# Turning the attention probabilities of layer 2: TensorE transposes replaced by 32x32 squares on VectorE and transfers within SBUF

## The chip, the cores and the metric

The kernel runs on one core of a Trainium2 chip, in one launch. A core has five engines that run side by side, each through its own instruction list in order: TensorE (PE in the profile, with PEld for its weight loads), VectorE (DVE), ScalarE (ACT), GpSimd (POOL) and SyncE (SP, which here only issues DMA transfers). An engine waits when an instruction needs a result of another engine or of a transfer. The metric is the device time of one execution in microseconds (us); of three runs of the kernel before, the median is 1385.75 us (1385.43 to 1386.89).

## What is computed

Four blocks, one after the other, on a residual stream x of 4 x 256 tokens of 512 floats. Each block normalises x and adds an attention and a feed-forward part to it. All is 32-bit floats. The change concerns the attention of block 2 alone:

```python
def _L2_attn_ref(hidden_states, Wqkv, Wo):       # 4 x 256 tokens, 32 query heads, 8 key heads, 128 wide
    qkv = jnp.einsum('bsh,oh->bso', hidden_states, Wqkv)
    ...
    xq = _apply_rope(xq, cos, sin)
    xk = _apply_rope(xk, cos, sin)
    ...
    scores = jnp.einsum('bqhd,bkhd->bhqk', xq, xk) * scale
    scores = jnp.where(causal, scores, -1e30)
    probs = jax.nn.softmax(scores, axis=-1)
    out = jnp.einsum('bhqk,bkhd->bqhd', probs, xv)
    return jnp.einsum('bsd,hd->bsh', out, Wo)

xn = _layernorm(x)
x = x + _L2_attn_ref(xn, Wqkv, Wo) + _L2_ffn_ref(xn, ...)
```

## The kernel before, in words

The work of blocks 2 and 3 is written as a list of tasks for TensorE (`layers_2_and_3`). One task is a group of eight 128x256 float matmul passes (two passes for each matmul that the program names). Seven tasks make a product of 2x2 blocks by seven multiplications (`seven`): four PSUM banks X, Y, Z and W are opened by tasks 0 to 3, and tasks 4 to 6 add to three of them. Around each group ScalarE copies two banks out (`u` at line 1330, `z` at 1335), and VectorE adds them together (1332, 1340, 1350) and either rotates queries and keys (1411, 1413; GpSimd adds the halves at 1420) or adds to the residual stream (1454).

There are sixteen rounds, called quads; a round makes the queries of the next quad (7 tasks), the output product of the one before (7 tasks) and in some rounds new keys and values (7 more tasks). In between, the attention of four units runs. A unit, here called a head h, is one key head with two query heads of one batch: 64 heads in all, each spread over m tasks, m being 3 to 6 and in the first rounds more. The helper `run` takes the tasks in order; each task is a slot, and `after(k, f)` puts an operation k slots later. All engines but SP keep exactly this written order (`manual_schedule`).

For head h, counted from its first slot:

- slot 0, before the task: `scores` puts four matmuls on TensorE (lines 1755, 1759): 128 later queries against 256 keys and 128 earlier queries against 128 keys, for both query heads.
- slot 0: `masked`, four VectorE instructions that add the causal mask, store the negated scores in SBUF and keep their extreme (line 1773).
- slot 1: `exponentials`, four ScalarE instructions (1789), in place.
- slot 2: `normalise`, a reciprocal on VectorE (1800) and two products on GpSimd (1803), in place.
- slot m//3 of the next head: `transposes`, six 128x128 transposes on TensorE into banks T and V (1811 to 1814), and `copies`, two ScalarE copies to SBUF (1821, 1822).
- slot 2m//3 of the next head: `values`, the product with the values (1828, 1829), and a slot later `gathered`, a ScalarE copy of the result to SBUF (1837).

The probabilities of later and earlier queries lie in two tiles, p1 and p0, of two buffers each; q0 and q1, their transposes, have one buffer each. Weights come by transfers that SP issues; the tile framework gives all transfers of SP and ScalarE eight completion counters in turn, and a transfer waits until the one before it on its counter has landed.

Of the kernel before, what the change touches and what calls it, by code (L numbers as in the profile page):

```python
# [21 lines left out]
F32 = mybir.dt.float32  # L22
# [9 lines left out]
P = 128  # L32
# [24 lines left out]
def block_stack(ctx: ExitStack, tc: tile.TileContext, d: dict, out: bass.AP):  # L57
# [1188 lines left out]
    def layers_2_and_3(w, late):  # L1246
# [8 lines left out]
        with ExitStack() as stack:  # L1255
# [229 lines left out]
            class Layer3:  # L1485
# [29 lines left out]
                def integers(self):  # L1515


                    self.held = xs.tile([P, NC, C], F16, name="w3_h")
                    pk = [lnp.tile([P, C], F32, tag="xn", name=f"pk_{a}").bitcast(I32) for a in range(2)]
                    for a in range(2):  # L1520
                        nc.sync.dma_start(out=pk[a], in_=d["pk3"][:, a, :])

                    def step(a, k):
                        q = sp.tile([P, C], I32, tag="p1", name="nib")
                        nc.vector.tensor_scalar(
                            q, pk[a], 4 * k, 15, ALU.logical_shift_right, ALU.bitwise_and
                        )
                        nc.vector.tensor_copy(self.held[:, 2 * a + k, :], q)

                    return [lambda a=a, k=k: step(a, k) for a in range(2) for k in range(2)]  # L1530
# [233 lines left out]
            def masked(h):  # L1764

                x = heads[h]
                x["p1"] = sp.tile([P, 2, T], F32, tag="p1", name="p1")
                x["p0"] = sp.tile([P, 2, P], F32, tag="p0", name="p0")
                for k in ("nm", "sums", "rs"):
                    x[k] = sp.tile([P, 2, 2], F32, tag=k, name=k)  # L1770
                for part in (1, 0):
                    for e in range(2):
                        nc.vector.tensor_tensor_reduce(  # L1773
                            out=x[f"p{part}"][:, e, :],
                            in0=x[f"s{part}"][:, e, :],
                            in1=cmask if part else cmask[:, P : 2 * P],
                            scale=-1.0,
                            scalar=-NEG,
                            op0=ALU.add,
                            op1=ALU.min,  # L1780
                            accum_out=x["nm"][:, part, e : e + 1],
                        )
# [15 lines left out]
            def normalise(h):  # L1798
                x = heads[h]
                nc.vector.reciprocal(x["rs"], x["sums"])  # L1800
                for part, n in ((1, T), (0, P)):
                    p = x[f"p{part}"]
                    nc.gpsimd.tensor_tensor(p, p, bc(x["rs"][:, part, :], 2, n), ALU.mult)  # L1803

            def transposes(h):


                x = heads[h]
                t0, t1 = ps("T", [P, 2, T], "pT0"), ps("V", [P, 2, P], "pT1")
                for i in range(2):  # L1810
                    nc.tensor.transpose(t0[:, i, 0:P], x["p0"][:, i, :], ident)
                    nc.tensor.transpose(t0[:, i, P:T], x["p1"][:, i, 0:P], ident)  # L1812
                for i in range(2):
                    nc.tensor.transpose(t1[:, i, :], x["p1"][:, i, P:T], ident)
                x.update(t0=t0, t1=t1)

            def copies(h):
                x = heads[h]
                x["q0"] = sp.tile([P, 2, T], F32, tag="q0", name="q0", bufs=1)
                x["q1"] = sp.tile([P, 2, P], F32, tag="q1", name="q1", bufs=1)  # L1820
                nc.scalar.copy(x["q0"], x["t0"])  # L1821
                nc.scalar.copy(x["q1"], x["t1"])  # L1822

            def values(h):
                x = heads[h]
                v = x["kt"][:, 1, :]
                av = x["av"] = ps("V", [P, 2, T], "av2")
                nc.tensor.matmul(av, lhsT=v[:, 0:P], rhs=x["q0"], start=True, stop=False)  # L1828
                nc.tensor.matmul(av[:, :, P:T], lhsT=v[:, P:T], rhs=x["q1"], start=False, stop=True)  # L1829

            attended = {}

            def gathered(h):
                x = heads.pop(h)
                i, j = x["c"]
                o = tile2("o", 8, f"o2_{h}")
                nc.scalar.copy(o, x["av"])  # L1837
                attended.setdefault(x["quad"], {})[f"a{i + 1}{j + 1}"] = o

            def piece(h, k, m):  # L1840


                if h >= 1 and k == m // 3:
                    transposes(h - 1)
                    copies(h - 1)
                if h >= 1 and k == 2 * m // 3:
                    values(h - 1)
                    after(1, lambda: gathered(h - 1))
# [14 lines left out]
            def run(tasks):  # L1863

                for task in tasks:
                    h, at, m = beats.pop(slot[0], (None, 0, 0))
                    if h is not None and at == 0 and h < 4 * QUADS:
                        scores(h)
                        after(0, lambda h=h: masked(h))
                        after(min(1, m - 1), lambda h=h: exponentials(h))  # L1870
                        after(min(2, m - 1), lambda h=h: normalise(h))
                    task()


# [446 lines left out]
```

## Time and profile before

| what | value |
|---|---|
| median of three runs | 1385.75 us |
| the profiled execution, its own time | 1389.1 us |
| its span from first to last instruction | 1387.2 us |
| TensorE busy, of the span | 1347.8 us (97%) |
| VectorE, ScalarE, GpSimd busy | 62%, 38%, 55% |
| stretch from 530 to 1250 us (attention of block 2): TensorE busy | 717.8 of 720 us |
| the same stretch: VectorE, ScalarE, GpSimd busy | 439.0, 265.8, 469.2 us |
| the two GpSimd products of line 1803, mean | 1067 and 653 ns |
| the two ScalarE copies of lines 1821 and 1822, mean | 585 and 377 ns |
| granted TensorE clock in this stretch | 1.00 |

A group of instructions in the profile is given with its line, its engine, its operation, what it writes and reads, its shape and count, the busy time of the group, the mean of one, and the idle time of the engine before it with what ended that. A timeline line starts with the time from the span's start and the duration, both in us; some neighbouring instructions are merged in it (x8). Matmuls overlap in the array, so the distance between starts, not the duration shown, is what one occupies. A PE line counts the passes of a float matmul, two for each; a transpose is one pass. Of a matmul the profile names the output, then the moving and the stationary tile.

### The profile page before, as it was taken

To read this page: it belongs to the slowest core of one execution; us is meant where nothing else is said; L and a number is where in the kernel's file an instruction comes from. 1 tells how busy PE (TensorE), PEld (TensorE's weight loads), DVE (VectorE), ACT (ScalarE), POOL (GpSimd) and SP (SyncE) were. 2 spreads that over 40 slices of the span, in tenths; PEclk is the share of its full clock that TensorE was granted. 3 is DMA by queue.
4 is the path that set the end of the run, shared out by engine and by line. 5 is a ranking of instruction groups with operands and counts; after the bars stand their busy time and mean duration, and the time that the engine had idled before them with its cause. 6 is when DMAs were issued, how large, how long until landed. Compare 5 with 4: busy or idle time off the path is not lost.

```text
span 1387.2 us, 20593 instructions
## 1 busy us (share of the span) xinstructions
PE 1347.8 (97%) x7460; PEld 1064.6 (77%) x7460; DVE 865.7 (62%) x1905; ACT 525.0 (38%) x1346; POOL 760.8 (55%) x782
## 2 busy tenths in 40 slices
PE   9899999899998999999999999999999999999998
PEld 7566665687445678888888888888888888877887
DVE  7576677488835358545665756655466655758654
ACT  2444435387012213323333333333333344555440
POOL 4455456477645025674776856868658675331410
PEclk9899999999999999999999999999999999999999
DMA  5022213200600022011311203121122000302001
GB/s 199 14 46 47 47 35 92 73 1 19 188 28 16 1 84 77 1 46 38 104 57 46 69 17 103 62 72 40 55 69 101 20 24 1 137 1 114 1 1 61
DMA packets 51317, 76.52 MB, mean 55 GB/s; under 512 B 16538, under 2 KB 24373, under 8 KB 50832
## 3 DMA queue, kind: packets, MB, share of 16 engines
q1 hardware_dynamic: 50288, 74.16, 17.2%
q8 instruction: 59, 0.97, 0.3%
q10 hardware_dynamic: 816, 0.79, 0.2%
q14 instruction: 42, 0.34, 0.1%
q0 software_dynamic: 112, 0.26, 0.1%
HBM read 67.28 MB, written 7.91 MB: 54 GB/s over the span
## 4 chain that ended last, share of the span: by engine, by line
PE 90%; DVE 6%; ACT 2%; issue 1%; POOL 1%; DVEq 0%; ACTq 0%; POOLq 0%
PE m L1396 18%; PE m L1360 15%; PE gu L782 6%; PE dn L745 5%; PE half L287 4%; PE s L1755 4%; PE av L1828 4%; PE m L1382 3%; PE m L1372 3%; PE half L327 2%; PE s L1759 2%; PE av L1829 2%; PE l1o L1033 2%; PE st L449 2%; PE s L386 2%; PE half L479 2%
## 5 line engine op out<-in xcount | busy, mean ns | idle before, releaser
L1803 POOL TENSOR_TENSOR p<-p,rs 128x512 f32<-128x512 f32 (+1 forms) x128 | 107.3, 860 | 147.2 <-DVE rs L1800 136.3
L1789 ACT ACTIVATE p<-p,nm 128x256 f32<-128x256 f32 (+1 forms) x256 | 113.3, 443 | 105.8 <-DVE nm L1773 105.5
L1454 DVE TENSOR_TENSOR x_sb<-x_sb,m 128x512 f32<-128x512 f32 x82 | 56.0, 686 | 82.4 <-PE m L1396 67.3
L1360 PE MATMUL m<-xT,wq_b 128*128 128x256 f32 x448 | 103.9, 380 | 2.5 <-ACT kv L1445 1.4
L1773 DVE CUSTOM_DVE_ANT_0 p<-s,cmask 128x256 f32<-128x256 f32 (+1 forms) x256 | 76.2, 354 | 47.5 <-PE s L1755 45.4
L1420 POOL TENSOR_TENSOR q<-q,t 128x512 f32<-128x512 f32 x64 | 82.2, 1285 | 31.4 <-DVE t L1411 28.1
L1837 ACT COPY o<-av 128x512 f32<-128x512 f32 x64 | 37.5, 586 | 156.5 <-PE av L1829 156.5
L1360 PEld LDWEIGHTS m<-xT,wq_b 128*128 128x128 f32 x448 | 82.1, 190 | 13.0 <-ACT kv L1445 1.8
L1396 PE MATMUL m<-wo_b,o 128*128 128x256 f32 x384 | 89.6, 379 | 0.0
L1411 DVE TENSOR_TENSOR t<-m,rope_sb 64x512 f32<-64x512 f32 (+1 forms) x144 | 86.3, 599 | 2.1 <-POOL q L1420 0.2
L463 POOL TENSOR_SCALAR_AFFINE_SELECT keys<-keys 128x256 f32<-128x256 f32 x128 | 56.7, 452 | 49.9 <-ACT keys L459 43.5
L1343 POOL TENSOR_TENSOR c<-c,z 128x512 f32<-128x512 f32 x28 | 36.5, 1302 | 86.6 <-DVE c L1340 45.9
L1821 ACT COPY q<-pT 128x512 f32<-128x512 f32 x64 | 37.5, 585 | 122.3 <-PE pT L1812 122.2
L802 POOL TENSOR_TENSOR sa<-sa,sb 128x1024 f32<-128x1024 f32 x22 | 62.0, 2823 | 30.7 <-DVE sb L797 30.7
L1396 PEld LDWEIGHTS m<-wo_b,o 128*128 128x128 f32 x384 | 71.3, 190 | 8.8
L745 PE MATMUL dn<-wd,hT 128*128 128x512 f32 x176 | 76.4, 593 | 0.7 <-ACT o L741 0.7
L1360 PE MATMUL m<-x_s,wq_t 128*128 128x256 f32 x320 | 75.4, 380 | 1.2 <-ACT kv L1445 1.1
L459 ACT ACTIVATE keys<-st 128x384 f32<-128x384 f32 x128 | 55.9, 487 | 40.0 <-PE st L449 40.0
L1360 PEld LDWEIGHTS m<-x_s,wq_t 128*128 128x128 f32 x320 | 59.8, 190 | 10.1 <-ACT kv L1445 1.5
L1828 PE MATMUL av<-q,kv 128*128 128x512 f32 x128 | 65.6, 594 | 0.6 <-ACT q L1822 0.6
L1755 PE MATMUL s<-kv,q 128*128 128x256 f32 x256 | 65.8, 379 | 0.0
L745 PEld LDWEIGHTS dn<-wd,hT 128*128 128x128 f32 x176 | 33.2, 190 | 41.1 <-issue 39.5
(337 smaller groups left out, 3448.0 us busy)
## 6 DMA issues: line engine op xcount, KB each, us to landing
wq_b<-in_wq SPq DMA_DIRECT2D x38, 256.0 KB, 3.1
wo_b<-in_wo SPq DMA_DIRECT2D x32, 256.0 KB, 2.6
raw<-in_wo SPq DMA_DIRECT2D x16, 512.0 KB, 3.6
wkv_b<-in_wkv SPq DMA_DIRECT2D x16, 256.0 KB, 2.6
wos_d<-wos_row SPq DMA_DIRECT2D x28, 128.0 KB, 2.7
gate_q<-in_gate_q SPq DMA_DIRECT2D x11, 256.0 KB
up_q<-in_up_q SPq DMA_DIRECT2D x11, 256.0 KB
wq3s_b<-in_wq SPq DMA_DIRECT2D x8, 256.0 KB, 3.1
```

Of the source, the lines that this page charges most:

```text
L745: nc.tensor.matmul(po, lhsT=hT[:, k, t * P : (t + 1) * P], rhs=wd[:, k, :], start=k == 0, stop=k == NBLK - 1,)
L782: nc.tensor.matmul(p[:, half], lhsT=w[:, g, :], rhs=x[half][:, g], start=k == 0, stop=k == 1,)
L802: nc.gpsimd.tensor_tensor(self.a, self.a, self.b, ALU.add)
L1360: nc.tensor.matmul(out[:, i, :], lhsT=b[:, c, i * P : (i + 1) * P], rhs=a[:, c, :], start=start and i == 0 and c == 0, stop=i == 1 and c == 1,
L1396: nc.tensor.matmul(out[:, t, :], lhsT=a[:, c, t * P : (t + 1) * P], rhs=b[:, c, :], start=start and t == 0 and c == 0, stop=t == 1 and c = ...
L1411: nc.vector.tensor_tensor(t2[at], src[of], sin[of], ALU.mult)
L1420: after(1 + 2 * pause, lambda: nc.gpsimd.tensor_tensor(dst, dst, t2, ALU.add))
L1755: nc.tensor.matmul(s1[:, i, :], lhsT=q[:, i, P:T], rhs=kt[:, 0, :], start=True, stop=True)
L1773: nc.vector.tensor_tensor_reduce(out=x[f"p{part}"][:, e, :], in0=x[f"s{part}"][:, e, :], in1=cmask if part else cmask[:, P : 2 * P], scale ...
L1789: nc.scalar.activation(p, p, AF.Exp, bias=x["nm"][:, part, e : e + 1], scale=-1.0, accum_out=x["sums"][:, part, e : e + 1],)
L1803: nc.gpsimd.tensor_tensor(p, p, bc(x["rs"][:, part, :], 2, n), ALU.mult)
L1828: nc.tensor.matmul(av, lhsT=v[:, 0:P], rhs=x["q0"], start=True, stop=False)
```

## The change

The probabilities of a head are turned without TensorE:

- p0 and p1 become two views of one tile p with one buffer: for each of the two query heads 3 x 128 columns (earlier queries' 128 keys, later queries' 256 keys).
- `normalise` scales on ScalarE, four instructions with the reciprocal as a scale per partition, in place of two on GpSimd.
- `transposes` and `copies` go. `turned_blocks` takes their place: one VectorE instruction transposes 32x32 squares of the whole of p into a tile `blocks`, reading every fourth column, so that the four columns that will sit on neighbouring partitions end in four rows of one partition. Four transfers, issued by ScalarE, then move 32 partitions each to all 128 partitions of q, 768 bytes to a partition. It stands at slot max(3, 2m//3) of the head itself; for m = 3 that is the first slot of the next head.
- `values` reads q in its new order and writes the bank in an order of 32 columns; `gathered` puts the columns back in order.
- A scratch tile of the last block's weights (`nib`) uses the rotary's buffer t2, as tag p1 is gone.

```diff
-                        q = sp.tile([P, C], I32, tag="p1", name="nib")
+                        q = tile2("t2", 2, "nib").bitcast(I32).rearrange("p a i -> p (a i)")
...
-                x["p1"] = sp.tile([P, 2, T], F32, tag="p1", name="p1")
-                x["p0"] = sp.tile([P, 2, P], F32, tag="p0", name="p0")
+                p = x["p"] = sp.tile([P, 2, 3, P], F32, tag="p", name="p", bufs=1)
+                p = p.rearrange("p e x k -> p e (x k)")
+                x["p0"], x["p1"] = p[:, :, 0:P], p[:, :, P:]
...
                 nc.vector.reciprocal(x["rs"], x["sums"])
-                for part, n in ((1, T), (0, P)):
-                    p = x[f"p{part}"]
-                    nc.gpsimd.tensor_tensor(p, p, bc(x["rs"][:, part, :], 2, n), ALU.mult)
-
-            def transposes(h):
+                for part in (1, 0):
+                    for e in range(2):
+                        p = x[f"p{part}"][:, e, :]
+                        nc.scalar.activation(p, p, AF.Copy, scale=x["rs"][:, part, e : e + 1])
+
+            def turned_blocks(h):
                 x = heads[h]
-                t0, t1 = ps("T", [P, 2, T], "pT0"), ps("V", [P, 2, P], "pT1")
-                for i in range(2):
-                    nc.tensor.transpose(t0[:, i, 0:P], x["p0"][:, i, :], ident)
-                    nc.tensor.transpose(t0[:, i, P:T], x["p1"][:, i, 0:P], ident)
-                for i in range(2):
-                    nc.tensor.transpose(t1[:, i, :], x["p1"][:, i, P:T], ident)
-                x.update(t0=t0, t1=t1)
-
-            def copies(h):
-                x = heads[h]
-                x["q0"] = sp.tile([P, 2, T], F32, tag="q0", name="q0", bufs=1)
-                x["q1"] = sp.tile([P, 2, P], F32, tag="q1", name="q1", bufs=1)
-                nc.scalar.copy(x["q0"], x["t0"])
-                nc.scalar.copy(x["q1"], x["t1"])
+                blocks = sp.tile([P, 4, 6, 32], F32, tag="blocks", name="blocks", bufs=1)
+                nc.vector.transpose(
+                    blocks, x["p"].rearrange("p e x (i b) -> p b (e x) i", b=4)
+                )
+                q = x["q"] = sp.tile([P, 4, 6, 32], F32, tag="q", name="q", bufs=1)
+                for a in range(4):
+                    nc.scalar.dma_start(
+                        out=q[:, a].rearrange("k m j -> k (m j)"),
+                        in_=blocks[32 * a : 32 * a + 32].rearrange("i b m j -> i b (m j)"),
+                    )
...
-                av = x["av"] = ps("V", [P, 2, T], "av2")
-                nc.tensor.matmul(av, lhsT=v[:, 0:P], rhs=x["q0"], start=True, stop=False)
-                nc.tensor.matmul(av[:, :, P:T], lhsT=v[:, P:T], rhs=x["q1"], start=False, stop=True)
+                q = x["q"].rearrange("p a (e x) j -> p a e (x j)", e=2)
+                av = x["av"] = ps("V", [P, 4, 2, 64], "av2")
+                nc.tensor.matmul(av, lhsT=v[:, 0:P], rhs=q[:, :, :, 0:64], start=True, stop=False)
+                nc.tensor.matmul(
+                    av[:, :, :, 32:], lhsT=v[:, P:T], rhs=q[:, :, :, 64:], start=False, stop=True
+                )
...
-                nc.scalar.copy(o, x["av"])
+                nc.scalar.copy(
+                    o.rearrange("p e (x a j) -> p a (e x) j", x=2, a=4),
+                    x["av"].rearrange("p a e (x j) -> p a (e x) j", x=2),
+                )
...
-                if h >= 1 and k == m // 3:
-                    transposes(h - 1)
-                    copies(h - 1)
                 if h >= 1 and k == 2 * m // 3:
                     values(h - 1)
...
                         after(min(2, m - 1), lambda h=h: normalise(h))
+                        after(max(3, 2 * m // 3), lambda h=h: turned_blocks(h))
```

## The prediction

> **What bounds the kernel now.** I read the page first, then the busy time by stretch, then the waits, and last the timeline of the tightest heads. The page, and the table by stretch for the whole attention of block 2 (columns: stretch, length, then busy time and count of PE, PEld, DVE, ACT, POOL, clock, DMA share, GB/s):
>
> ```profile
> span 1387.2 us, 20593 instructions
> PE 1347.8 (97%) x7460; PEld 1064.6 (77%) x7460; DVE 865.7 (62%) x1905; ACT 525.0 (38%) x1346; POOL 760.8 (55%) x782
> ```
>
> ```profile
> 530.00:1250.00 720.00, 717.78 (x3704) 617.19 (x3703) 438.99 (x1114) 265.78 (x818) 469.22 (x435) 1.00 0.17 55
> ```
>
> TensorE works without a gap in this stretch; the others have 40% or so to spare. The waits of PE there sum to 2.2 us in three places, and the chain that ended last is PE for 90% of the span. So what leaves TensorE here leaves the time, as long as nothing else takes its place. The timeline of one head with m = 3 (start, duration):
>
> ```profile
> 1083.70 1.03 PE L1755 MATMUL s<-kv,q 128*128 128x256 f32 x4
> ...
> 1088.47 0.27 PE L1811 MATMUL pT<-ident,p 128*128 128x128 f32 x1
> 1088.58 0.27 PE L1812 MATMUL pT<-ident,p 128*128 128x128 f32 x1
> ...
> 1089.12 1.89 PE L1360 MATMUL m<-x_s,wq_t 128*128 128x256 f32 x8
> ...
> 1090.85 1.02 PE L1828 MATMUL av<-q,kv 128*128 128x512 f32 x2
> ...
> 1092.14 1.03 PE L1755 MATMUL s<-kv,q 128*128 128x256 f32 x4
> ```
>
> Starts tell what each occupies: six transposes 0.65 (1088.47 to 1089.12), a task 1.73 (1089.12 to 1090.85), values 1.29, the period 8.44, so scores are 8.44 - 0.65 - 3 x 1.73 - 1.29 = 1.31. Distances between scores over the whole trace are 8.4 (m = 3), 10.2 (m = 4), 11.9 and more. I call 30 heads tight: 20 that alternate 8.44 and 10.16, and 10 near the end, nine at 8.44 and one at 10.16; 272 us together. The other 34 have 11.5 or more, but for the first one.
>
> The prices, by line and shape (mean in ns of one):
>
> ```profile
> L1821 ACT COPY q<-pT 128x512 f32<-128x512 f32 x64 | 37.5, 585 | 122.3 <-PE pT L1812 122.2
> L1822 ACT COPY q<-pT 128x256 f32<-128x256 f32 x64 | 24.1, 377 | 0.0
> L1718 ACT ACTIVATE ret<-num,den 128x128 f32<-128x128 f32 x64 | 17.4, 383 | 24.7 <-DVE den L1712 24.7
> L1648 ACT ACTIVATE sig<-m,bq_sb 128x256 f32<-128x256 f32 x24 | 10.1, 478 | 5.0 <-DVE m L1350 3.9 <-PE m L1360 1.0
> L501 DVE STREAM_TRANSPOSE wd<-o 128x256 f32<-128x256 f32 x16 | 7.0, 435 | 0.5 <-POOL o L498 0.5
> wos_d<-wos_row SPq DMA_DIRECT2D x28, 128.0 KB, 2.7
> 765.99 0.81 SPq L2001 DMA_DIRECT2D wos_d<-wos_row  x2
> ```
>
> The first two go; the next two price the scaling, the fifth the squares, the last two a transfer out of SBUF (landing, and two issues).
>
> **The change, part by part.** *TensorE, removed:* 64 x 0.65 = 42 us, all on the path. *Values:* same columns, in pieces of 32; the kernel's other 128x256 and 128x512 rows price them alike, so 0. The worst row beside them, 667 ns for a 32x512 matmul against 594, would make it 12% of 64 x 1.29, 10 us.
>
> *GpSimd:* loses 110 us (68.3 + 41.8 of line 1803). TensorE never waits for it in this stretch, so this is worth 0.
>
> *ScalarE, per head:* loses 0.96 (both copies). Gains four scalings: 10.1 / 24 = 0.42 and 17.4 / 64 = 0.27 us each when back to back, 1.4 in sum (1.7 by the means). Gains four issues at 0.40 to 0.47, 1.85 in sum; ends 0.33 each (the shortest of SP) and 0.62 (ScalarE's own for a small load at the start), 1.3 to 2.5. The copy of line 1837 in another order: 0.59, at worst 0.86, the strided row of line 1562. Net +2.3 on 4.2 per head; over the stretch 266 becomes some 410 of 680. There is room, but the waits count, see below.
>
> *VectorE:* one transpose of 768 columns. From 435 ns for 256 and 265 more for each further 256 (line 1413: 425 and 690): 0.97. High end 1.3, three times the row, or 1.36 times for the step, as line 1562 with a step of two floats takes 857 against 632 for a plain pass of line 1657. I take 1.0. [...]
>
> *The transfers:* four of 96 KB. Landing 1.8 (128 KB stores at the end) to 3.6 us (512 KB loads); I take the 2.7 of the row out of SBUF, its nearest. In a tight head, from the start of scores: the reciprocal is done after 3.7 to 5.8 us (four heads from 1092 to 1125), scaling 1.4, squares 1.0 and up to 0.7 of queue, fourth issue 1.4 later, landing 2.7: 10.2 to 13.0. TensorE reaches these values after 1.31 + 5.19 + 1.29 + 1.31 + 5.19 = 14.3. So the transfer is hidden, with 1.3 to 4 us left; with m = 5 more than 5 are left.
>
> *New waits.* (a) A ring of VectorE and ScalarE. With p single, the masks of head h+1 stand behind the squares of h on VectorE; the exponentials of h+1 stand behind the four issues of h on ScalarE, which wait for the squares, which wait for the scalings. One turn: squares 1.0, issues 1.85, copy 0.59, exponentials 1.9 (1093.78 to 1095.65), reciprocal 0.17, scalings 1.4, four hand-overs of 0.1, a share of the u and z copies 0.25, waiting behind a rotary pair or an add on VectorE 0 to 1.4, taken 0.7: 8.3 us. Ends 6.8 and 10.5. TensorE now needs 7.78 (m = 3) or 9.51 (m = 4): the alternating heads average 8.64 and still cover the ring, the nine in a row do not: 9 x 0.5 = 5 us lost, and 3 in collisions elsewhere. (b) The order of the changed program with its waits shows 84 of ScalarE's 256 issues waiting also for an earlier transfer of SP on the same counter; 17 of those SP transfers hang on work that lies under 6.5 us of TensorE work back, 5 on work with none between, mostly GpSimd's sums of line 1990. Such a sum takes 1.27, SP's issue 0.43, the landing 2.7: ScalarE stands 4.4 us, and everything queued behind it, exponentials and the z copy that TensorE needs two tasks later. With half the slack above hiding 2.4: 5 x 2 = 10, the other twelve hidden. Ends 0 and 17 x 4.4 = 75. (c) Weight fetches share the transfer engines (0.17 busy): 2 us.
>
> *SP* waits now for ScalarE's counters too; by the programs' orders its fetches keep some 13 us or more of TensorE work, priced by the rows above, between the last thing they wait for and their first use, before and after alike: 0. *nib:* four instructions, 0.
>
> Sum: -42 + 5 + 3 + 10 + 2 = -22. The profiled execution took 1389.1 (span 1387.2, 1.9 around it), 0.24% above the median 1385.75. 1389.1 - 22 = 1367; on the median's scale 1385.75 - 22 = 1364, 1.6% faster.
>
> [...]
>
> **The rivals.**
> 1. *All hidden.* Ring and counters cost nothing: 1385.75 - 42 = 1344. For it: ScalarE now stands still for TensorE 156.5 us ahead of line 1837 and 122.2 ahead of 1821, so it has time to give. Against: the nine heads in a row have no cover.
> 2. *Slower: the ring becomes the bound.* Price: 30 tight heads at L us against 272, less 0.65 x 34 = 22 for the rest, plus 12 for (b) and (c). It decides from L = (272 + 22 - 12) / 30 = 9.4. At L = 10, 300 - 272 - 22 + 12 = +18: 1404. For it: three of its terms have no row of their own kind, and all high ends together give 10.5. Against: the middle is 8.3.
> 3. *Late landing.* If the four transfers end 6 us after the last issue instead of 2.7, the 1.3 to 4 us left become -2 to +0.7, one late us in the mean: 30 x 1 more, 1394. Against: no row of issues in the stretch lands later than 4.3.
>
> **How the numbers follow.** Forecast 0.55, all hidden 0.20, ring 0.16, late landing 0.07, other 0.02. What a measurement can tell from no change is 0.2%, 2.8 us. The forecast's own range, with (b) between 0 and 25, is 1353 to 1380. The whole range takes in all hidden and half of the slow cases: 1342 to 1400. Faster: forecast, all hidden and a little of the rest, 0.77; slower 0.19; same 0.04.
>
> **What the profile after would show.** No pT rows; the stretch near 680 to 700 us with PE over 95%; STREAM_TRANSPOSE of 128x768 near 1.0 us; the issues on ACT near 0.45; q landing under 4; PE's waits under 25 us, at the values and in the last tight heads. Wrong if the transpose is over 1.5 us, if scalings or issues on ACT wait in most heads, or if PE's waits for q exceed 40 us.

## The result, and the profile after

The changed kernel took 1396.85 us (median of four runs, 1395.35 to 1397.70) against 1386.32 for the kernel before on the same chip (four runs, 1385.43 to 1388.06): a ratio of 1.0069, 95% interval 1.0056 to 1.0081. It is 10.5 us slower; 1364 was forecast. In the experiments below, times stand beside runs of the kernel before on their own chips, which had medians of 1386.9 to 1387.8.

The profiled execution took 1395.35 us. Its page, first the span and the engines' busy time:

```profile
span 1393.6 us, 20495 instructions
PE 1319.3 (95%) x7076; PEld 1028.6 (74%) x7076; DVE 948.3 (68%) x1969; ACT 556.3 (40%) x1474; POOL 656.7 (47%) x654
```

TensorE has 384 instructions fewer and 28.5 us less work, not the 42 that were taken out; and the span is 6.4 longer, so its idle time rose from 39.4 to 74.3 us. Why the work fell by 28.5 only is taken up below, at the clock.

The groups of the changed operations on the page, and its row for the transfers (kilobytes, and us from issue to landing):

```profile
L1813 DVE STREAM_TRANSPOSE blocks<-p 128x768 f32<-128x768 f32 x64 | 101.1, 1579 | 20.7 <-ACT p L1805 19.3
L1841 ACT COPY o<-av 128x512 f32<-128x512 f32 x64 | 37.7, 589 | 189.9 <-DMA q<-blocks 53.0
L1805 ACT ACTIVATE p<-p,rs 128x256 f32<-128x256 f32 (+1 forms) x256 | 95.5, 444 | 38.1 <-DVE rs L1801 38.1
...
q<-blocks ACTq DMA_DIRECT2D x256, 96.0 KB, 2.4
```

The squares took 1.58 us, not 1.0. The four scalings took 1.49, near the 1.4 forecast (it is the distance of start and end of the four; the mean of one overlaps). The copy of line 1841 costs what it cost before (589 ns), but its row has 189.9 us of idle time ahead of it, in which ScalarE issues the transfers or waits at them. The view of the one line that issues the transfers (minimum, median and maximum of one in ns):

```profile
L1818 ACTq DMA_DIRECT2D q<-blocks x256: 550/625/1233, 539.1 to 1245.1; - x128
L1818 ACTq EVENT_SEMAPHORE  x190: 17/38/5949, 536.0 to 1240.6; - x190
```

An issue holds ScalarE for 0.63 us, not 0.46; four are 2.52, not 1.85. ScalarE's queue also waits ahead of issues. The longest wait, 5.9 us at head 47, ended with VectorE's squares (they were done at 1078.53, the first issue went out at 1078.61), so no transfer was behind it. The stretch from 530 to 1250 us, in the columns of the table before, and TensorE's waits from 530 to 1300 us (sum, times, longest, in us):

```profile
530.00:1250.00 720.00, 682.61 (x3270) 574.65 (x3270) 511.65 (x1162) 293.82 (x937) 362.73 (x305) 0.98 0.33 89
```

```profile
PE av L1830 <- DMA q<-blocks: 13.3, 5, 5.9
PE av L1830 <- ACT p L1790: 5.7, 3, 2.5
PE m L1372 <- ACT z L1335: 5.0, 7, 3.2
PE m L1396 <- DVE o_s L1099: 4.2, 1, 4.2
PE lnT L148 <- ACT xn L1562: 2.8, 3, 2.1
PE m L1396 <- DVE x_sb L1454: 2.6, 3, 1.3
```

The transfer reaches TensorE late eight times only, 19.0 us in all: the second line is such waits too (at head 35 the last transfer was issued at 937.33 and landed near 940.3, and TensorE started at 940.65). In five of the eight the landing took the usual 2.3 to 2.5 us, so the transfers had gone out late. The six lines sum to 33.6 us. So the loss is not one thing in every head. To place it I took the distance between the scores of one head and the next in both traces (each the start of its first matmul of line 1755), and call **growth** what the distance after has over the distance before less 0.65 (the transposes). If all were hidden, every head would have a growth of 0. The sum over the 63 distances is 50.4 us; 63 x 0.65 = 41.0 were removed, so this stretch became 9.4 longer (3.0 came back outside it). It is in lumps:

| where | growth, us |
|---|---|
| three single heads: 19 (7.6), 29 (5.1), 35 (4.4) | 17.2 |
| heads 54 to 60 and 62, in and after the streak with m = 3 | 11.0 |
| head 61 | 6.2 |
| the other 51 distances, none over 2.7 | 16.1 |

The three single heads in the timeline (start and duration in us, then engine and line; in brackets the idle time before, and what ended it). Head 29, ScalarE, SP and TensorE, three answers:

```profile
863.32 5.55 ACTq L1818 DMA_DIRECT2D q<-blocks  x4
868.92 0.59 ACT L1335 COPY z<-m 128x512 f32<-128x512 f32 x1 [10.10 <-DMA raw<-in_wo]
```

```profile
862.43 0.80 SPq L2006 DMA_DIRECT2D wos_d<-wos_row  x2
863.29 0.44 SPq L1986 DMA_DIRECT2D raw<-in_wo  x1
```

```profile
865.74 0.61 PE L1759 MATMUL s<-kv,q 128*128 128x128 f32 x4
869.55 1.37 PE L1372 MATMUL m<-x_s,wkv_b 128*128 128x256 f32 x4 [3.20 <-ACT z L1335]
```

ScalarE did nothing from 858.8 to 868.9. Two waits make this up. The squares were done at 860.78, but q has one buffer, and TensorE finished reading the q of the head before at 863.28; the first issue went out at 863.32. Then the four took 5.55 instead of 2.52, as ScalarE stood 3.0 us among them for transfers of SP on the same counters, the last of them issued at 863.29; the z copy that releases a bank to TensorE stood behind. The second is the wait (b) of the prediction, and this is the only head in which it shows: in all others the four issues take 2.5 to 3.1 us. Head 19 is another kind:

```profile
757.08 1.89 PE L1396 MATMUL m<-wo_b,o_s 128*128 128x256 f32 x8
764.83 2.04 PE L1830 MATMUL av<-q,kv 128*128 128x512 f32 x2 [5.87 <-DMA q<-blocks]
766.67 1.06 PE L1831 MATMUL av<-q,kv 128*128 128x256 f32 x2
```

Here the transfers went out from 756.24 to 759.05, into SP's fetch of four 256 KB weights, and landed 5.7 us after the issue instead of 2.4. The table by stretches of 4 us shows the load, and the clock after the wait (last columns: granted clock, DMA share, GB/s):

```profile
756.00:760.00 4.00, 2.97 (x14) 2.28 (x12) 3.87 (x13) 0.91 (x3) 0.46 (x1) 1.00 0.96 208
760.00:764.00 4.00, 0.00 (x0) 0.00 (x0) 3.93 (x7) 2.93 (x12) 4.00 (x5) 0.64 0.89 313
764.00:768.00 4.00, 3.17 (x6) 1.91 (x7) 3.38 (x5) 0.00 (x0) 4.00 (x4) 0.51 0.03 9
768.00:772.00 4.00, 4.00 (x22) 3.59 (x21) 3.16 (x11) 1.55 (x5) 4.00 (x5) 1.00 0.68 189
```

After the gap the granted TensorE clock was 0.51, and the values took 2.04 where they take 1.02. This wait was paid for again afterwards. Over the whole execution: the same 7076 TensorE instructions are busy for 1306.7 us where nearly nothing waits (the run without transfers and with two buffers, below) and for 1319.3 here. So of the loss 12.6 us is longer TensorE work, and 34.9 is idle time: 1306.7 - 1347.8 + 12.6 + 34.9 = +6.4, the change of the span. The clock is some 8 us of the 12.6 at most, an estimate from its means (0.990 over 1393.6 us against 0.996 over 1352.1 in that run); the rest is not placed.

Head 35 is a third kind, late squares. From the scores of head 34 to the wait at its values, in the lists of TensorE, VectorE and ScalarE:

```profile
923.75 1.03 PE L1755 MATMUL s<-kv,q 128*128 128x256 f32 x4
932.08 0.16 DVE L1801 RECIPROCAL rs<-sums 128x4 f32<-128x4 f32 x1
933.81 1.55 DVE L1813 STREAM_TRANSPOSE blocks<-p 128x768 f32<-128x768 f32 x1 [0.99 <-ACT p L1805]
935.44 2.53 ACTq L1818 DMA_DIRECT2D q<-blocks  x4
940.65 1.10 PE L1830 MATMUL av<-q,kv 128*128 128x512 f32 x2 [2.48 <-ACT p L1790]
```

The exponentials ended 5.6 us after the scores began, where they ended after 3.5 before the change, because the masks stood in VectorE's list behind the squares of the head before and its sums and rotation of queries. Then the reciprocal stood 2.7 us behind the next rotation. So it was done after 8.5 us (4.0 before the change) and the squares after 11.6, and TensorE, which was at the values after 14.4, waited 2.5. Heads 18, 22, 38 and 50 have the same order and the same lateness; in all five TensorE waited, for 1.7 to 5.9 us, and head 18 is the one whose values head 19 waits for.

One more wait shows in the wide heads, here head 25:

```profile
823.75 1.58 DVE L1813 STREAM_TRANSPOSE blocks<-p 128x768 f32<-128x768 f32 x1
826.89 0.59 PE L1831 MATMUL av<-q,kv 128*128 128x256 f32 x2
827.52 2.52 ACTq L1818 DMA_DIRECT2D q<-blocks  x4
```

The squares were done at 825.33, and ScalarE stood until TensorE had read the q of the head before, at 827.48. So it is in 23 of the 64 heads, mostly those with m of 4 and more, for 0.5 to 2.6 us each, 39.1 us in sum. What it costs in the end was not tried alone: no run has two buffers of q.

### The profile page after: what moved, and what is told of

Same layout as the page of the kernel before. It is cut to its first block, busy times and chain, and to the rows that moved or that the text cites. A ratio compares the mean times of both kernels' runs of the same rounds, so it can differ in the third digit from the quotient of the medians.

```text
span 1393.6 us, 20495 instructions
## 1 busy us (share of the span) xinstructions
PE 1319.3 (95%) x7076; PEld 1028.6 (74%) x7076; DVE 948.3 (68%) x1969; ACT 556.3 (40%) x1474; POOL 656.7 (47%) x654
## 5 line engine op out<-in xcount | busy, mean ns | idle before, releaser
L1813 DVE STREAM_TRANSPOSE blocks<-p 128x768 f32<-128x768 f32 x64 | 101.1, 1579 | 20.7 <-ACT p L1805 19.3
L1841 ACT COPY o<-av 128x512 f32<-128x512 f32 x64 | 37.7, 589 | 189.9 <-DMA q<-blocks 53.0
L1805 ACT ACTIVATE p<-p,rs 128x256 f32<-128x256 f32 (+1 forms) x256 | 95.5, 444 | 38.1 <-DVE rs L1801 38.1
L1099 POOL TENSOR_TENSOR o_s<-o,o 128x512 f32<-128x512 f32 x14 | 17.8, 1272 | 147.4 <-ACT o L1841 119.0
L1360 PEld LDWEIGHTS m<-x_s,wq_t 128*128 128x128 f32 x320 | 60.3, 190 | 10.5 <-ACT kv L1445 1.5
```

The costliest lines, as they stand in the source:

```text
L1360: nc.tensor.matmul(out[:, i, :], lhsT=b[:, c, i * P : (i + 1) * P], rhs=a[:, c, :], start=start and i == 0 and c == 0, stop=i == 1 and c == 1,
L1805: nc.scalar.activation(p, p, AF.Copy, scale=x["rs"][:, part, e : e + 1])
L1813: nc.vector.transpose(blocks, x["p"].rearrange("p e x (i b) -> p b (e x) i", b=4))
```

## The experiments

Theory A: the loss is a few collisions of the transfers with SP's fetches (ScalarE held at an issue, or a landing behind a fetch). Theory B: the ring of VectorE and ScalarE is longer than TensorE's work in the tight heads. All edits are against the changed kernel unless it says otherwise.

### Without the transfers

```diff
-                q = x["q"] = sp.tile([P, 4, 6, 32], F32, tag="q", name="q", bufs=1)
-                for a in range(4):
-                    nc.scalar.dma_start(...)
+                x["q"] = blocks
```

> Left out: the four transfers of a head; the values' matmuls read the squares' result (blocks) directly, so the probabilities reach the wrong partitions. Everything else of the change stays. Theory A (the 53 us that went missing of the removed 42 + what was lost come from the transfers: their four issues on ScalarE, what ScalarE waits for ahead of them, and their late landing): all of it comes back but a few us for the slower squares, 1344 to 1352 us. Theory B (the ring of VectorE and ScalarE is too long even without them, through squares of 1.58 us and scalings of 1.49 us): the ring falls from about 8.4 to about 5.9 us, under every head's TensorE work, so B gives nearly the same, 1344 to 1355. Rival C (the new order of the values' matmuls, of the copy out of their bank, or the other places outside the heads cost time by themselves): 1360 or more. This run sets the floor that the others are measured from.

Measured: 1376.96 us, ratio 0.9930 (0.9915 to 0.9944). The number is in the third expectation's "1360 or more", but not for its reason, as the waits of VectorE say:

```profile
DVE blocks L1813 <- PE av L1826: 105.8, 44, 4.1
```

The edit had made a wait of its own: blocks has one buffer, and now TensorE read it, so the squares of a head stood until the values of the head before, and VectorE's adds behind them. It shows what 106 us of waits on VectorE cost (22.5 us more than the run after next, which has none of them), but it is no floor. The next has the same flaw:

```diff
-                q = x["q"] = sp.tile([P, 4, 6, 32], F32, tag="q", name="q", bufs=1)
+                x["q"] = blocks
+                q = sp.tile([P, 4, 6, 32], F32, tag="q", name="q", bufs=1)
```

> Left out: the values read the squares' result (blocks), not the tile q that the transfers fill; the four transfers of a head are still issued and still land. So TensorE never waits for a landing, but ScalarE still pays the issues and stands at them. If late landing behind the weight fetches is the larger part of the loss (theory A1): 1355 to 1370. If ScalarE's time at the issues is (theory A2: 0.63 us each, and waits of up to 5.9 us for an SP transfer on the same counter): 1385 to 1396, with TensorE waiting for the z copy of line 1335 and for the exponentials. Theory B (length of the ring): 1390 or more as well, with the loss spread over all tight heads rather than in three or four lumps.

Measured: 1437.46, 1.0366 (1.0350 to 1.0381). Only theory B's "1390 or more" covers it, but not for B's reason: VectorE waited at the squares for TensorE again (42.1 us), now with ScalarE's issues behind them. It tells nothing on landing. (The waits of up to 5.9 us in the expectation were put down to SP's transfers; the longest was for VectorE's squares, as said above.) Both flaws go with a second buffer, for which there was room only without q:

```diff
-                blocks = sp.tile([P, 4, 6, 32], F32, tag="blocks", name="blocks", bufs=1)
+                blocks = sp.tile([P, 4, 6, 32], F32, tag="blocks", name="blocks", bufs=2)
```

> The first experiment again without its own new wait: there the squares of a head stood on VectorE until TensorE had read the squares of the head before (105.8 us of waits at the transpose), because blocks has one buffer. Here blocks has two buffers and q none. Left out: the four transfers of a head; the values read blocks, so the probabilities reach the wrong partitions. If the transfers are the whole of what went missing (removed 42 us, none of it lost otherwise): 1344 to 1350 us. If the values' new order, the scalings or the squares still cost TensorE: 1355 to 1377.

Measured: 1354.43, 0.9762 (0.9747 to 0.9776). Growth 9.4 in sum: 0.0 at the three heads, 0.3 at 54 to 60 and 62, 2.2 elsewhere, and 6.9 at head 61. So scalings, squares, the values' new order and the copy out of their bank are hidden but for 2.5 us everywhere but at head 61, and 41 of the 50 us come from the transfers or from what they do to the ring. The floor is 1354 and not 1344, between the two expectations; of these 10 us head 61 is 7.

### One part undone: the scaling on GpSimd

```diff
-                for part in (1, 0):
-                    for e in range(2):
-                        p = x[f"p{part}"][:, e, :]
-                        nc.scalar.activation(p, p, AF.Copy, scale=x["rs"][:, part, e : e + 1])
+                for part, n in ((1, T), (0, P)):
+                    p = x[f"p{part}"]
+                    nc.gpsimd.tensor_tensor(p, p, bc(x["rs"][:, part, :], 2, n), ALU.mult)
```

> One part undone: the probabilities are scaled by GpSimd's two products again (1.07 and 0.65 us in the trace of before), and ScalarE's four scalings (1.49 us a head) go. Theory B (ring length decides): the chain from the reciprocal to the squares is 0.2 us longer, but ScalarE is 1.49 us a head freer, so the tight heads lose less: 1375 to 1388. Theory A (few collisions at the issues): the issues and the landings stay where they are, within 5 us of the changed kernel, 1391 to 1402.

Measured: 1418.35, 1.0228 (1.0213 to 1.0243): 21 us slower than the changed kernel, against B and A. The waits of VectorE from 530 to 1250 us:

```profile
DVE blocks L1812 <- POOL p L1804: 58.5, 38, 6.7
```

The two products stand in GpSimd's list behind its adds, and VectorE now stands in line for them: 58.5 us at the squares, up to 6.7 at once, where the scalings on ScalarE cost it 19.3. I had counted ScalarE's time alone and not what queue the products stand in. Against this alternative the scaling on ScalarE pays.

### The squares without a step

```diff
-                    blocks, x["p"].rearrange("p e x (i b) -> p b (e x) i", b=4)
+                    blocks, x["p"].rearrange("p e x (b i) -> p b (e x) i", b=4)
```

> Changed: the VectorE transpose reads 32 neighbouring columns for each square in place of every fourth column; same count, same size, same transfers, but the probabilities reach the wrong partitions. The estimate from rows of the trace of before was 0.97 us for plain squares of 768 columns; the changed kernel took 1.58 with a step of four floats. If the step is what costs: about 1.0 us and, by theory B (0.6 us off each turn of the ring), 8 to 25 us less than the changed kernel: 1372 to 1389. By theory A: under 5 us less, 1392 to 1398. If the step isn't what costs, the row stays near 1.58 and so does the time.

Measured: 1383.75, 0.9981 (0.9967 to 0.9994), ten runs from 1380.7 to 1389.2.

```profile
L1813 DVE STREAM_TRANSPOSE blocks<-p 128x768 f32<-128x768 f32 x64 | 62.5, 977 | 21.2 <-ACT p L1805 19.2
```

0.98 us against 1.58: the step of four floats (16 bytes) is the whole of the error in that term, and the estimate of 0.97 for plain squares was right. The 0.60 us a head gave 13.1 us: growth fell at heads 54 to 60 and 62 (11.0 to 6.2) and elsewhere (16.1 to 9.8), and not at the three heads (17.2 to 16.2). That is theory B for these two, and not for the three heads as a whole.

### SP issues the transfers

```diff
-                    nc.scalar.dma_start(
+                    nc.sync.dma_start(
```

> One change: SP issues the four transfers of a head in place of ScalarE, in the same written place. Theory B (length of the ring: of 8.4 us a turn the four issues are 2.52): the ring falls to about 5.9 us and a landing is 0.1 us later; the sum of the prediction with no ring and no ScalarE issues is 1344 + 2 to 10: 1346 to 1360. Theory A (collisions with SP's weight fetches): SP's list is in order, so the transfers now wait for whatever fetch stands ahead of them, and the fetches wait for the squares: the lumps stay or grow, 1380 to 1410.

Measured: 1367.47, 0.9848 (0.9829 to 0.9867), 29.4 us faster than the changed kernel and between the two expectations, of which neither covers it. Growth 21.8: 2.4 at the three heads, 3.1, 10.9 at head 61, 5.3 elsewhere. The issue costs SP nearly what it costs ScalarE (0.60 and 0.63 us), where SP's own issues of lines 1986 and 2006 had medians of 0.33 in the changed kernel's trace. So the price goes with the transfer and not with the engine:

```profile
L1818 SPq DMA_DIRECT2D q<-blocks x256: 542/601/1657, 542.6 to 1217.7; - x128
```

Both theories had a reason for this, so the next run gives ScalarE the time of the issues back, without their waits. Built on this kernel:

```diff
+                for a in range(4):
+                    nc.scalar.copy(ps("T", [P, 2, T], "spare"), blocks[...])   # 512 columns
```

> Built on the kernel in which SP issues the transfers (1367.5 us, 29.4 less than the changed kernel). ScalarE gets four copies of 128x512 from blocks into an unused PSUM bank at the written place of its four issues, about 2.4 us a head back to back where the issues took 2.52; nobody reads what they write. So ScalarE has the time of the issues back, but not their waits for an SP transfer on the same counter. Theory B (ScalarE's plain time in the ring): most of the 29 us comes back, 1385 to 1397. Theory A (ScalarE stands at the issues for transfers of SP): little comes back, 1367 to 1375. A value between says what share each has.

Measured: 1379.50, 0.9947 (0.9930 to 0.9963), between the two.

```profile
L1817 ACT COPY spare<-blocks 128x512 f32<-128x512 f32 x256 | 151.0, 590 | 143.9 <-DVE blocks L1813 137.8
```

Time on ScalarE (4 x 0.59 = 2.36) brings back 12.0 of the 29.4 us, and the growth shows where: heads 54 to 60 and 62 from 3.1 to 7.6, elsewhere 5.3 to 10.6, the three heads 2.4 to 2.5. By another division, the tight heads (m = 3, or 3 and 4 in turn; without 19 and 35) grew by 15.1 us in the changed kernel, 7.4 with SP issuing and 16.4 with the copies; the rest (without 29 and 61) by 12.0, 1.0 and 1.8. So in the tight heads the time of the issues on ScalarE, and with it the length of the ring, is enough for the whole loss; in the others it brings almost nothing back, and what they lost has to do with where ScalarE stands for the transfers. Its wait for the one buffer of q fits this, but was not tried alone. The three heads, too, need the transfers in ScalarE's list. To test these three alone, SP issues for six heads and ScalarE for 58:

```diff
-                    nc.scalar.dma_start(
+                    (nc.sync if h in (18, 19, 28, 29, 34, 35) else nc.scalar).dma_start(
```

> The changed kernel, but SP issues the transfers of six heads only (18, 19, 28, 29, 34, 35), those in front of the three places where a single head grew by 7.6, 5.1 and 4.4 us; ScalarE issues the other 58 as before. Theory A for these places (ScalarE stands at an issue whose counter an SP transfer holds, or the transfers go out into SP's burst from a second queue): these lumps, 17 us in all with SP issuing everywhere shrinking to 2, shrink as far here, 1379 to 1386. If the lumps come from the length of the ring in the heads around them: 1392 to 1397, since 58 of 64 heads keep it. If the order of the counters decides and moves with the few: lumps of the same size at other heads, 1388 to 1400.

Measured: 1388.58, 1.0010 (0.9995 to 1.0025), its ten runs spread from 1385.3 to 1395.4: 8 us better than the changed kernel, just short of A's range. It lies in the third expectation's range, but its lumps did not move to other heads. In its profiled execution (1386.95) head 29's lump is gone, head 35's went from 4.4 to 1.9, and head 19's only from 7.6 to 6.3; the other rows stayed (11.3, 6.1, 15.3). So A holds for 29. At head 35 the squares were as late as before; TensorE waited 1.7 us instead of 2.5, and the clock was 1.00 in the two stretches of 4 us behind it, where it had been 0.75 and 0.82. At head 19 SP now issued the transfers ahead of the fetch, they landed after 3.1 us instead of 5.7, TensorE waited 3.3 instead of 5.9, and then ran at a clock of 0.76, 0.50 and 0.89 in three stretches of 4 us. With SP issuing everywhere the squares there came earlier, and head 19 grew by 1.2. Its cause is then a late start (B) that meets a burst; how they divide stays open.

### The scaling on VectorE

```diff
-                        nc.scalar.activation(p, p, AF.Copy, scale=x["rs"][:, part, e : e + 1])
+                        nc.vector.tensor_scalar(p, p, x["rs"][:, part, e : e + 1], None, ALU.mult)
```

> One change: the four scalings go from ScalarE to VectorE, straight ahead of the squares, which need them there. ScalarE's four took 1.49 us; a VectorE tensor_scalar of 128x512 took 0.50 us in the changed kernel (line 1654), so four of 256 and 128 columns are put at 0.27 x 2 + 0.17 x 2 = 0.9 us. Theory B: the turn of the ring is 0.7 us shorter with one hand-over less; by the plain squares' rate (0.60 us a turn off gave 13.1 us) about 15 us less than the changed kernel, 1376 to 1386. Theory A: within 5 us of it, 1391 to 1401. Against both: VectorE gets 0.9 us a head more, and the adds on TensorE's banks stand behind it: at the most 1405.

Measured: 1477.28, 1.0639 (1.0622 to 1.0657), far from all expectations. VectorE's part of the timeline, two heads, and GpSimd's beside the second:

```profile
1035.88 1.01 DVE L1805 TENSOR_SCALAR p<-p,rs 128x256 f32<-128x256 f32 x4
1045.18 4.62 DVE L1805 TENSOR_SCALAR p<-p,rs 128x256 f32<-128x256 f32 x4
```

```profile
1042.75 1.28 POOL L1099 TENSOR_TENSOR o_s<-o,o 128x512 f32<-128x512 f32 x1 [13.61 <-ACT o L1841]
1043.98 1.28 POOL L1343 TENSOR_TENSOR c<-c,z 128x512 f32<-128x512 f32 x1
1045.20 1.28 POOL L1099 TENSOR_TENSOR o_s<-o_s,o 128x512 f32<-128x512 f32 x1
1046.43 0.79 POOL L1420 TENSOR_TENSOR kv<-kv,t 128x256 f32<-128x256 f32 x1
1047.18 1.31 POOL L1103 TENSOR_TENSOR o<-o,o 128x512 f32<-128x512 f32 x1
```

The four take 1.01 us when GpSimd is idle and up to 4.62 when it works. Of the 56 groups of four that the timeline shows together, the 24 at 1.01 have no GpSimd instruction beside them, and the others last longer, the more of one they overlap (1.44 with 0.63 to 0.64 us of it, 3.5 to 4.6 where GpSimd works nearly throughout). What makes them longer beside it, the rows do not show. My price of 0.50 us was the mean of 16 rows of line 1654, of which most had no GpSimd work beside them (their median is 0.41); the longest, 1.18, had.

### The plain squares made right, by a step in TensorE's operand

```diff
+                keys = kt[:, 0, :].rearrange("p (x i b) -> p x b i", x=2, b=4)
...
-                        s1[:, i, :], lhsT=q[:, i, P:T], rhs=kt[:, 0, :], start=True, stop=True
+                        s1[:, i, :], lhsT=q[:, i, P:T], rhs=keys, start=True, stop=True
...
-                    blocks, x["p"].rearrange("p e x (i b) -> p b (e x) i", b=4)
+                    blocks, x["p"].rearrange("p e x (b i) -> p b (e x) i", b=4)
```

> The plain squares with the computation whole: TensorE reads the keys in the order of every fourth token when it makes the scores (a step of four floats in its moving operand), and the causal mask lies in the same order, so the squares can read neighbouring columns and the transfers put everything where it belongs. If TensorE reads with the step as fast as without: the squares take 0.98 us and the time is that of the plain squares, 1380 to 1389. If the step costs TensorE as it cost VectorE (1.6 times on the 64 x 1.31 us of the scores, 50 us): 1425 to 1445.

Measured: 1439.00, 1.0367 (1.0350 to 1.0385).

```profile
L1764 PE MATMUL s<-kv,q 128*128 128x256 f32 x256 | 125.9, 625 | 0.0
```

625 ns against 379 before: the step of 16 bytes costs TensorE 1.65 times in its moving operand, and that on the engine that sets the time. Nearly every head grew by 1.4 us (heads 0, 19, 61 and 62 by 2.0 to 3.4). With TensorE that much slower the ring costs next to nothing: TensorE's waits from 530 to 1300 us are 6.5 us in all.

### Laid out once, and the last heads

Here the keys are laid out in that order when they are rotated, 32 times in all, and TensorE reads them without a step. SP issues.

```diff
+                nc.vector.tensor_tensor(turned(dst), plain(src), plain(cos), ALU.mult)
...
+                    nc.vector.tensor_tensor(
+                        turned(t2[at]), plain(src[of]), plain(sin[of]), ALU.mult
+                    )
...
-                    blocks, x["p"].rearrange("p e x (i b) -> p b (e x) i", b=4)
+                    blocks, x["p"].rearrange("p e x (b i) -> p b (e x) i", b=4)
...
-                    nc.scalar.dma_start(
+                    nc.sync.dma_start(
```

> A version meant to beat both: SP issues the transfers, and the squares read neighbouring columns, which is made right by laying the rotated keys out once, when they are made (32 groups of three VectorE products write every fourth token together; the mask in the same order; TensorE reads the keys without a step). By the single changes: SP 29.4 and plain squares 13.1 us off 1396.85 if they add: 1354; as the ring no longer binds once the issues are off ScalarE, the squares' share may fall to 2 to 5 us: 1354 to 1366. If VectorE's scattered writes cost 1.6 times, 96 x 0.25 us on an engine 69% busy, mostly hidden: at the most 1370.

Measured: 1361.82, 0.9818 (0.9797 to 0.9839). Growth 13.9, of which head 61 has 11.5: in all other heads together 2.4 us are left. The same with GpSimd's queue in place of SP's:

```diff
-                    nc.sync.dma_start(
+                    nc.gpsimd.dma_start(
```

> As the one with the keys laid out, but GpSimd's queue issues the transfers (GpSimd is 47% busy and SP's list of weight fetches is left alone). No row shows what an issue costs there. At 0.5 us or less each, and with the transfers no longer behind a weight fetch in SP's list: 1346 to 1360. At 1.2 us or more each GpSimd gets 5 us a head, its adds for the c banks and the sums of the output products fall behind and SP's fetches with them: 1380 to 1420.

Measured: 1424.19, 1.0267 (1.0234 to 1.0300).

```profile
L1844 POOL DMA_DIRECT2D q<-blocks x256 | 140.2, 568 | 208.5 <-PE av L1857 126.5
```

An issue costs GpSimd 0.57 us, just over the cheap case (0.5 or less), and still the outcome is the dear one, even 4 us above its range: the price is that GpSimd's list stands still ahead of the issues, 208.5 us, of which 126.5 until TensorE has read q (it has one buffer), with GpSimd's adds behind. Last, head 61 of the version with SP, where the transfers of head 60 stood behind SP's fetches:

```diff
-                    nc.sync.dma_start(
+                    (nc.sync if h < 60 else nc.scalar).dma_start(
```

> The version with the keys laid out and SP issuing, 1361.8 us, but ScalarE issues for the last four heads (60 to 63). There head 61 alone grew by 11.5 us: the transfers of head 60 stood in SP's list behind fourteen fetches of the last block's weights, from the squares' end at 1162.6 to 1167.6, and landed at 1174.5 (TensorE waited 6.3 us). Without transfers at all head 61 still grew by 6.9. If SP's list is the cause of the difference: 4 to 6 us less, 1355 to 1358. If the late landing comes from the weight fetches filling the transfer engines, whoever issues: 1359 to 1363.

Measured: 1356.61, 0.9777 (0.9762 to 0.9791), 5 us less, as the list of SP would have it; head 61 grew by 6.6 instead of 11.5. This is the fastest version, 2.2% under the kernel before, and 2 us over the floor without transfers. What TensorE still waits for in it, 530 to 1300 us, the first three:

```profile
PE m L1404 <- DVE o_s L1107: 3.8, 1, 3.8
PE m L1404 <- DVE x_sb L1480: 1.9, 2, 1.3
PE w L1631 <- DVE x_sb L1480: 1.7, 1, 1.7
```

The first is head 61: VectorE's sums for an output product wait for ScalarE's copy of the heads' result. In this trace the copy stands at 1166.2, behind scalings and issues, where TensorE had finished the values at 1159.8; before, it started 0.04 us after them. That this order is the cause was not tried.

## Why the prediction was wrong, point by point

Growth by place, in us, in the traces of the kernels that this rests on:

| kernel | sum | heads 19, 29, 35 | 54 to 60, 62 | 61 | elsewhere |
|---|---|---|---|---|---|
| changed kernel | 50.4 | 17.2 | 11.0 | 6.2 | 16.1 |
| plain squares | 37.7 | 16.2 | 6.2 | 5.6 | 9.8 |
| SP issues | 21.8 | 2.4 | 3.1 | 10.9 | 5.3 |
| SP issues, copies on ScalarE | 31.4 | 2.5 | 7.6 | 10.7 | 10.6 |
| six heads on SP | 40.9 | 8.2 | 11.3 | 6.1 | 15.3 |
| no transfers, two buffers | 9.4 | 0.0 | 0.3 | 6.9 | 2.2 |
| keys laid out, SP, last on ScalarE | 9.6 | 0.6 | 1.8 | 6.6 | 0.6 |

- *TensorE, removed, 42 us:* right. Without stalls the same instructions are busy for 1306.7 instead of 1347.8, 41.1 less.
- *Values, 0; GpSimd, 0; the copy out of the bank, 0:* right. The run without transfers shows all three hidden but for 2.5 us outside head 61, and the copy took 589 ns in its new order.
- *ScalarE, scalings 1.4:* right (1.49). *Issues 1.85:* too small (2.52). The rows that I took, 0.40 to 0.47, were of SP's transfers of another shape; the high end of the range, 0.62, came from ScalarE's own row and was the right one.
- *VectorE, squares 1.0, at worst 1.3:* too small and outside its bounds (1.58). The row that I scaled had no step; by plain squares the scaling is exact. No row that I had showed this step, and I took the bound from a ScalarE row with another one (857 against 632 ns).
- *Landing 2.7:* right in the median (2.4), and 5.7 at head 19. *"Hidden, with 1.3 to 4 us left"* failed ahead of heads 19, 23, 35, 39 and 51: the sum took the reciprocal's time from the profile before (3.7 to 5.8 us after the scores), and in the changed kernel it was done after 8.5, behind the ring's own delay on VectorE.
- *New waits (a), the ring, 8.3 us a turn, 5 + 3 lost:* this is the step that failed: squares put at 1.0 and issues at 1.85, and so a turn that TensorE covers in all but nine heads. With 1.58 and 2.52 in its sum, a turn is 8.3 + 0.58 + 0.67 = 9.55, past the 9.4 from which the second rival decides, and by that rival's sum 30 x 9.55 - 272 - 22 + 12 = +4.5 us. Measured is 27 us (heads 54 to 62 without 61, and elsewhere) for the 8 forecast. 11 of them go when 0.6 us of the squares go, and 19 when the issues leave ScalarE. But the mechanism is not quite the rival's: the heads of the streak at the end did not all run at the ring's length. Their distances were 7.8, 8.4, 10.2, 9.4, 7.8, 8.2, 8.7 and 10.5 (heads 53 to 60; TensorE's work alone is 7.78), that is, TensorE runs on what is ready, then loses 2 us at once, and a lower clock after that (0.78 and 0.80 in the two stretches of 4 us behind the wait of 2.1 us before head 56). Of the 27 us 15.1 are in the tight heads and belong to the ring's length, which the time given back to ScalarE shows; 12.0 are outside them, where the prediction had 3 for collisions. There plain squares took 4.0 off, and ScalarE's wait for the one buffer of q, which the sum put at nothing by leaving it out, is the likely rest, not shown.
- *(b), counters, 10 us:* the mechanism is shown at head 29 alone (3.0 us of ScalarE's time, a growth of 5.1). Of the 17.2 us at the three heads 14.7 go when SP issues everywhere, even with ScalarE's time given back, and 9.0 when it issues for the six heads only. But heads 19 and 35 are no counter: they are late squares, met by a burst and a lower clock. That 17.2 lies near the 10 + 2 foreseen is luck.
- *(c), weight fetches, 2 us:* not seen by itself; it is in head 19 and in part in head 35, whose transfers landed after 5.7 and 3.1 us beside a fetch.
- *SP, 0:* held with ScalarE issuing. With SP issuing, its list cost 5 us at head 61.
- *Left out:* head 61, 6.2 us, and 5.6 to 11.5 in every version but the one with the step in TensorE's operand; its cause was not tried. And the clock, some 8 us at most: I had named a wait as costing its length.

The sum by what was measured: -41.0 + 27.1 (the ring, and the heads outside it) + 17.2 (three heads) + 6.2 (head 61) = +9.5 against -22. Of the 31.5 us between them 19.1 are in the first (27.1 against 5 + 3), 5.2 at the three heads (17.2 against 10 + 2), 6.2 at head 61 and 1.0 in what was removed. Of the announced signs of error the transpose over 1.5 us appeared; issues on ScalarE did wait in most heads, for the squares or for TensorE's reading of q; TensorE's waits for q did not exceed 40 us (19.0), since most of the loss shows as waits for ScalarE and VectorE, and as longer TensorE work. The stretch did not become shorter, and TensorE was busy for 95% of it all the same, so that sign told nothing.

The second rival named the right side and the right cause at 0.16. What should have moved its chance: three of the ring's terms had no row of their kind, and the middle of the sum, 8.3 us, was already past the 7.78 of nine heads and only 0.3 under the 8.64 of the alternating ones. Two of those terms then missed in the same direction.

## What to carry to other kernels

When work leaves the engine that sets the time, sum the turn of those that take it over, with a price from a row of the same access pattern and the same transfer shape; where none has it, decide by the high end if the cover is under a microsecond. A transfer belongs in the list of an engine that has nothing else to do for those who wait: its issue costs the issuer (0.57 to 0.63 us here), and its waits hold all that stands behind it (3.0 us of ScalarE's time at head 29, 208.5 us of GpSimd's in sum). Count the buffers that a transfer overwrites as well: with one, its issue stands until the last reader is done (0.5 to 2.6 us in 23 of the 64 heads). A layout that one engine must read with a step is better made once, where it is written (with SP issuing, 1361.82 us so, against 1367.47 with VectorE reading with the step).

## What the runs showed that was not expected

- A step of 16 bytes costs VectorE's squares 1.58 against 0.98 us, and TensorE's moving operand 625 against 379 ns.
- Behind waits of TensorE the granted clock in stretches of 4 us was 0.51 (after 5.9 us, head 19), 0.57 (3.2, head 29), 0.75 and 0.82 (2.5, head 35) and 0.78 (2.1, before head 56); behind one of 2.5 us (head 51) it stayed at 1.00. With the same 7076 instructions, TensorE's busy time was 1306.7 us in the run without transfers and with two buffers, 1319.3 in the changed kernel and 1342.8 with the scaling on VectorE, the slowest run.
- VectorE's tensor_scalar took longer beside GpSimd's work: the four 1.01 us alone, up to 4.62 beside it. Its squares took 1.55 to 1.61 us in all 64 heads of the changed kernel.
- Issuing the same transfer costs 0.63 us on ScalarE, 0.60 on SP and 0.57 on GpSimd.
